# A Mamba group's exponential, logarithm and sum of time steps, each moved one step in a tile pipeline

## The chip, the cores and the metric

One core of one Trainium2 chip runs the whole program. The metric is device time in microseconds. Lower is better.

The core has five engines with queues of their own, each working in order: PE (matrix products, with weight loads "PEld" beside it), DVE (vector operations), ACT (activation functions and copies), POOL (elementwise work and indirect DMAs) and SP (which here only issues DMAs).

## The reference

The program is a decoder of two layers on x of shape 16 x 100 x 256, with a context of 16 x 361 x 192. Layer 0: retention, cross attention, a mixture of 8 experts. Layer 1: Mamba, cross attention, an int8 product. The change lies in the Mamba part:

```
xz = x @ W_in                      # 256 -> z 2048, x 2048, B 64, C 64, dt 32
conv = depthwise causal convolution of width 4 over x, B, C, then silu
dt = softplus(dt_proj + dt_bias)   # per token and head, 32 heads
A = -exp(A_log)
h = exp(A * dt) * h + dt * x_t * B_t        # per head, over 100 tokens
y = C_t . h + D * x_t
y = norm_w * rmsnorm(y * silu(z));  return y @ W_out
```

softplus(v) is computed as max(v, 0) + log(1 + exp(-|v|)). With u = exp(-|v|) and w = 1 + u, the kernel takes log(w) and corrects it by u / (w - 1), with a guard for w = 1.

## The kernel before

**Groups and tiles.** The 16 sequences are 4 groups of 4, so 400 tokens. A group's 2048 inner channels are 16 tiles of 128 channels (2 heads). The loop at L1536 runs over n, from 0 to 72; a tile's group is n // 16, its index i is n % 16. The recurrence is computed as a masked product: per head, a 100 x 100 matrix L of exp of differences of running sums of A * dt, times the products B . C, times dt * x.

**The pipeline.** Within the block that opens at L1514 the order of PE, ACT, DVE, POOL and SP is that of the Python text: what is written first is queued first, on each engine. In step n, in this order: `closing` (end of the group before, i from 5 to 8), `gated` of tile n-4 (POOL, L1387), `rows_of` of tile n+2 (SP reads L's rows, L1316), `exponents` of tile n+1 (POOL, L1324 and L1325), `squares` of tile n-5 (POOL, L1398), `weights` of tile n-2 (DVE, L1332), `project` of tile n (PE L155, ACT L1199, DVE L1204 three times), `silu` of tile n (ACT, L1353 for z, L1354 for x), `exps` of tiles n and n+1 in even steps (ACT, L1328), `square` of tile n-4 (ACT, L1392), `turn` of tile n-2 (PE L1361, DVE `xdt` L1365), `result` of tile n-3 (PE L1379, DVE `y` L1384), `out` of tile n-5 (PE L1407), then `fetch` and `between`. The product `mm` has two PSUM buffers: one for x's half of the projection, one for z's.

**The next group's start.** `between` (L1473) prepares group g+1 in steps of group g, with one PSUM tile `st` for all of it:
- i = 7, 8: `start_x` turns x.
- i = 9: `start_dt` (L1237): PE makes the time steps' projection; DVE adds the bias (`dt_v`, L1248) and takes -|v| (`dt_u`, L1252); ACT takes its exponential (L1253); DVE adds 1 (`dt_w`, L1254); ACT takes the logarithm (`dt_ln`, L1255).
- i = 10: `start_sum` (L1271): eight DVE operations of 100 x 128 (L1274 to L1282), which end in `dt` and `dta` = dt * exp(A_log). Then `start_bc` for B (L1258): a PE product into `st`, an ACT step (L1199 on `bct`) and three DVE operations (L1204 on `bct`) that read `st`.
- i = 11: `start_rows` (L1286): four PE products (L1288) of `dta` with a triangle of ones into `st`, an ACT copy (L1292), a write to DRAM by SP (L1294) that `rows_of` later reads.
- i = 12: `start_cols` (L1296), i = 13: `start_bc` for C, i = 14: silu of B and C.

Group 0 has no group before it: its start runs ahead of the loop (L1515 to L1535).

**Activation tables.** ACT works from a table of functions that a load instruction puts in place; the compiler sets these loads where the function changes. A trace shows them as ACT_TABLE_LOAD under the line of the activation behind them.

Of the kernel before, what the change touches and what calls it, by code (L numbers as in the profile page):

```python
# [33 lines left out]
NG = B // G  # L34
# [48 lines left out]
def bc(ap, axis, n):  # L83

    v = ap.unsqueeze(axis)
    shape = list(v.shape)
    shape[axis] = n
    return v.to_broadcast(shape)


class Net:
# [1116 lines left out]
    def mamba(self, pool, w_out, w_x1):  # L1208
# [10 lines left out]
        one = lambda tag: self.psum.tile([P, 512], F32, tag=tag, name=tag, bufs=1)  # L1219
        xTs, dts, cols, das, gms, ssqs, accs = {}, {}, {}, {}, {}, {}, {}  # L1220
        xcs, szs, xdts, ls, ys, y2s = {}, {}, {}, {}, {}, {}
        st, mid, bct, rows_in, moe, ends = {}, {}, {}, {}, {}, {}
# [3 lines left out]
        def start_x(g, k):  # L1226
            if k == 0:
                st[g] = one("st")
                xTs[g] = pool.tile([P, 2, GT], F32, tag="xT", name="xT")
            for b in range(G):  # L1230
                nc.tensor.transpose(
                    st[g][:, b * T : (b + 1) * T], self.x[g][:, b, k * P : (k + 1) * P],
                    self.ident(T),
                )
            nc.scalar.copy(xTs[g][:, k, :], st[g][:, :GT])

        def start_dt(g):  # L1237

            pd = st[g][:T, :]
            for b in range(G):
                self.mm(
                    pd[:, b * 32 : (b + 1) * 32],
                    [(xTs[g][:, k, b * T : (b + 1) * T], self.w_in[:, k, 4224:4256]) for k in range(2)],
                )
            v, u, w, one, ln = (tile_(f"dt_{n}") for n in ("v", "u", "w", "one", "ln"))
            nc.vector.tensor_tensor(  # L1248
                v, pd[:, : 32 * G].rearrange("t (b h) -> t b h", b=G), bc(self.row("dt_bias"), 1, G),
                ALU.add,  # L1250
            )
            nc.vector.scalar_tensor_tensor(u, v, -1.0, v, ALU.mult, ALU.min)  # L1252
            nc.scalar.activation(u, u, AF.Exp)  # L1253
            nc.vector.tensor_scalar(w, u, 1.0, None, ALU.add)  # L1254
            nc.scalar.activation(ln, w, AF.Ln)  # L1255
            mid[g] = v, u, w, one, ln

        def start_bc(g, j):  # L1258

            lo_w, lo_b = PV["bc_w"][0], PV["bc_b"][0]  # L1260
            pc, at = st[g][:64, :GT], 4096 + 64 * j
            self.mm(pc, [(self.w_in[:, k, at : at + 64], xTs[g][:, k, :]) for k in range(2)])
            acc = pool.tile([64, GT], F32, tag=f"bc{j}", bufs=1, name="bct")
            self.conv(
                acc, pc,
                lambda k: self.pv[:64, lo_w + 4 * j + k : lo_w + 4 * j + k + 1],
                self.pv[:64, lo_b + j : lo_b + j + 1],
            )
            bct[j] = acc

        def start_sum(g):  # L1271

            v, u, w, one, ln = mid.pop(g)
            nc.vector.tensor_scalar(one, w, 1.0, None, ALU.is_equal)  # L1274
            nc.vector.scalar_tensor_tensor(w, w, -1.0, one, ALU.add, ALU.add)
            nc.vector.tensor_tensor(ln, ln, one, ALU.add)
            nc.vector.reciprocal(w, w)
            nc.vector.tensor_tensor(ln, ln, w, ALU.mult)
            nc.vector.tensor_tensor(ln, ln, u, ALU.mult)
            dt, dta = tile_("dt", 2), tile_("dta")  # L1280
            nc.vector.scalar_tensor_tensor(dt, v, 0.0, ln, ALU.max, ALU.add)
            nc.vector.tensor_tensor(dta, dt, bc(self.exp_a, 1, G), ALU.mult)  # L1282
            dts[g] = dt
            return dta

        def start_rows(g, dta):  # L1286
            for b in range(G):
                nc.tensor.matmul(  # L1288
                    st[g][:32, b * T : (b + 1) * T], dta[:, b, :], upper, start=True, stop=True
                )  # L1290
            rows = pool.tile([32, GT], F32, tag="dt_rows", bufs=1, name="dt_rows")
            nc.scalar.copy(rows, st[g][:32, :GT])  # L1292
            das[g] = tc.dram_tile([32, GT], F32, name=f"sums{g}")
            nc.sync.dma_start(das[g], rows)  # L1294

        def start_cols(g, dta):  # L1296
            pc = st[g][:T, : G * 32]
            nc.tensor.matmul(pc, upper, dta.rearrange("t b h -> t (b h)"), start=True, stop=True)
            cols[g] = tile_("cols", 2)
            nc.scalar.copy(cols[g], pc.rearrange("t (b h) -> t b h", b=G))  # L1300
# [12 lines left out]
        def rows_of(n):  # L1313
            g, i = divmod(n, 16)
            ls[n] = pool.tile([T, 2, G, T], F32, tag="L", bufs=7, name="L")
            nc.sync.dma_start(  # L1316
                ls[n].rearrange("s h b t -> s h (b t)"),
                das[g][2 * i : 2 * i + 2, :].unsqueeze(0).to_broadcast([T, 2, GT]),
            )
# [10 lines left out]
        def weights(n):  # L1330
            g = n // 16
            nc.vector.tensor_tensor(ls[n], ls[n], bc(gms[g], 1, 2), ALU.mult)  # L1332
# [53 lines left out]
        def gated(n):  # L1386
            nc.gpsimd.tensor_tensor(ys[n], ys[n], szs.pop(n), ALU.mult)  # L1387
# [85 lines left out]
        def between(n):  # L1473

            g, i = divmod(n, 16)
            if g + 1 >= NG:
                return
            if i == 5:
                moe[1] = self.moments(moe[0])
            if i == 6:  # L1480
                self.normalize(moe[0], *moe[1])
                self.x[g + 1] = moe[0]
            if i == 7:
                start_x(g + 1, 0)
            if i == 8:
                start_x(g + 1, 1)
            if i == 9:
                start_dt(g + 1)
            if i == 10:
                moe[2] = start_sum(g + 1)  # L1490
                start_bc(g + 1, 0)
            if i == 11:
                start_rows(g + 1, moe[2])
            if i == 12:
                start_cols(g + 1, moe[2])
            if i == 13:
                start_bc(g + 1, 1)
            if i == 14:
                silu_bc()

        def silu_bc():
            for j in range(2):
                nc.scalar.activation(bct[j], bct[j], AF.Silu)

        def closing(n):
            g, i = divmod(n, 16)
            if 1 <= g <= NG and 5 <= i < 9:
                (end_sums, end_add, end_moments, end_norm)[i - 5](g - 1)
# [5 lines left out]
        with tc.manual_schedule(engines={E.PE, E.Activation, E.DVE, E.Pool, E.SP}):  # L1514
            start_x(0, 0)  # L1515
            start_x(0, 1)
            start_dt(0)
            dta = start_sum(0)
            project(0)
            start_rows(0, dta)  # L1520
            start_cols(0, dta)
            for n in range(3):
                rows_of(n)

            self.load_mamba_out(w_out)
            silu(0)
            for j in range(2):
                start_bc(0, j)
                project(1 + j)
                silu(1 + j)  # L1530
            silu_bc()
            for n in range(2):
                exponents(n)
            for n in range(-4, 0):
                fetch(n)  # L1535
            for n in range(n_tiles + 9):  # L1536
                within = lambda k: 0 <= n - k < n_tiles
                closing(n)
                if n % 16 == 2 and n < n_tiles:
                    start_gm(n // 16)  # L1540
                if within(4):
                    gated(n - 4)
                if n >= 1 and within(-2):
                    rows_of(n + 2)
                if n >= 1 and within(-1):
                    exponents(n + 1)
                if within(5):
                    squares(n - 5)
                if within(2):
                    weights(n - 2)  # L1550
                if n >= ahead and within(0):
                    project(n)
                    silu(n)
                if n % 2 == 0 and within(0):
                    exps(n)
                    exps(n + 1)
                if within(4):
                    square(n - 4)
                if 4 <= n < 20:
                    scale_out(n - 4)  # L1560
                if n == 6:
                    self.load_cross1(w_x1)
                if within(2):
                    turn(n - 2)
                if within(3):
                    result(n - 3)
                if within(5):
                    out(n - 5)
                fetch(n)
                between(n)  # L1570
# [465 lines left out]
```

## Time and profile before

| | us |
|---|---|
| median of 3 runs (lowest, highest) | 2004.35 (2004.33, 2005.26) |
| the profiled execution | 2004.99 |
| its span | 2003.1 |
| Mamba's last output products (L1407) end | 1267.5 |
| PE busy in the span | 1800.7 |
| ACT busy in the span | 976.4 |
| POOL busy in the span | 683.9 |
| ACT_TABLE_LOAD, mean of one | 1.283 |
| ACT_TABLE_LOAD at L1253 and at L1255 | 4 each |
| ACT_TABLE_LOAD at L1353, at L1328 | 35, 31 |

A row of a timeline reads: start (us from the span's start), duration (us), engine, line, operation, out<-in, shapes, number of merged instructions, and in brackets how long the engine stood idle before it and what released it. A row of a table by stage reads: stretch, its length, then for PE, PEld, DVE, ACT and POOL the busy time and the number of instructions, then PE's granted clock as a share of full speed, the DMA engines' busy share and GB/s.

### The profile page before, as it was taken

The page shows a single profiled execution, that of the slowest core. Times are in us where ns is not written, and L with a number is a line of the kernel's source. Part 1 is how long each engine was busy: PE and PEld are TensorE (multiplying, and loading weights), DVE is VectorE, ACT ScalarE, POOL GpSimd, SP SyncE. Part 2 cuts the span into 40 slices and gives each one's busy share as a digit, 9 for nine tenths or more (in the row PEclk, how much of TensorE's full clock was granted, in tenths as well). Part 3 has the DMA queues.
Part 4 walks back from the last instruction along what each step waited for, and adds up shares of the span by engine and source line. Part 5 has one row for each costly group of instructions (what it writes and reads, how often), then busy time and mean ns, then how long its engine had stood idle before and what let it go on. Part 6 is the DMA issues. An engine that isn't in the chain of part 4 may idle for free. (4 is left out here: it accounts for less than half of the span.)

```text
span 2003.1 us, 31924 instructions
## 1 busy us (share of the span) xinstructions
PE 1800.7 (90%) x12268; PEld 1063.4 (53%) x12268; DVE 1124.8 (56%) x2466; ACT 976.4 (49%) x2294; POOL 683.9 (34%) x501
## 2 busy tenths in 40 slices
PE   6998999999949996799898998899999999999985
PEld 3556556555626663455555555445555555555553
DVE  3454577777632222687878867354446535444554
ACT  5732477667612221577667677333343433344343
POOL 2222232434320001558576566222222322322231
PEclk9999999999869998799999999999999999999997
DMA  4700600101023111422111110000000000000000
GB/s 148 311 1 1 230 24 16 31 26 33 16 87 135 45 45 33 121 103 80 41 57 52 47 52 33 21 16 8 9 8 16 17 8 8 9 16 15 1 9 9
DMA packets 46848, 96.98 MB, mean 48 GB/s; under 512 B 5844, under 2 KB 25940, under 8 KB 44266
## 3 DMA queue, kind: packets, MB, share of 16 engines
q1 hardware_dynamic: 41642, 83.75, 12.3%
q0 software_dynamic: 5056, 11.20, 1.8%
q8 instruction: 98, 1.61, 0.3%
q14 instruction: 52, 0.43, 0.1%
HBM read 69.48 MB, written 25.44 MB: 47 GB/s over the span
## 5 line engine op out<-in xcount | busy, mean ns | idle before, releaser
L1686 POOL TENSOR_TENSOR s<-s,den 100x1444 f32<-100x1444 f32 x64 | 165.9, 2593 | 509.5 <-DVE den L1685 467.7
L1677 ACT ACTIVATE s<-sc,top 100x361 f32<-100x361 f32 x256 | 140.3, 561 | 181.4 <-DVE top L1672 173.4
L155 PE MATMUL mm<-xT,w_mamba_in 128*128 128x400 f32 x512 | 203.2, 542 | 23.2 <-ACT sz L1353 18.9
L605 ACT COPY pT<-tr 128x400 f32<-128x400 f32 (+1 forms) x192 | 94.1, 494 | 190.6 <-PE tr L602 190.2
L1204 DVE SCALAR_TENSOR_TENSOR xc<-mm,pv,xc 128x388 f32<-128x388 f32 (+2 forms) x192 | 119.9, 625 | 80.1 <-ACT xc L1199 75.0
L739 POOL TENSOR_SCALAR w_experts<-w_experts 100x1444 f32<-100x1444 f32 x64 | 88.9, 1388 | 213.8 <-DVE w_experts L735 162.4
L1672 DVE TENSOR_REDUCE top<-sc 100x2 f32<-100x722 f32 x128 | 110.2, 902 | 88.5 <-PE sc L1667 88.5
L747 ACT ACTIVATE w_experts<-w_experts,top 100x361 f32<-100x361 f32 x256 | 149.3, 586 | 21.5 <-POOL w_experts L739 21.3
L155 PEld LDWEIGHTS mm<-xT,w_mamba_in 128*128 128x128 f32 x512 | 100.4, 204 | 107.0 <-ACT sz L1353 27.4
L605 DVE COPY pT<-tr 128x400 f32<-128x400 f32 x192 | 105.1, 569 | 56.7 <-PE tr L602 49.2
L735 DVE TENSOR_SCALAR_CACHE_REDUCE w_experts<-sc 100x361 f32<-100x361 f32 x256 | 121.2, 529 | 14.2 <-PE sc L729 13.5
L602 PEld LDWEIGHTS tr<-cn,s 100*128 100x128 f32 (+1 forms) x768 | 76.1, 154 | 88.5 <-issue 64.4
L1648 DVE COPY v<-mm 128x512 f32<-128x512 f32 (+1 forms) x96 | 61.9, 686 | 107.3 <-PE mm L595 107.3
L155 PE MATMUL sc<-w_experts,e_xT 128*128 x256 | 118.1, 605 | 2.2 <-DMA e_x<-rows 2.2
L602 PE MATMUL tr<-cn,s 100*128 100x100 f32 (+1 forms) x768 | 99.2, 266 | 18.5 <-DVE pT L605 18.5
L1387 POOL TENSOR_TENSOR y<-y,sz 128x400 f32<-128x400 f32 x64 | 67.5, 1055 | 134.1 <-DVE y L1384 103.0
L602 PE MATMUL tr<-cn,w_experts 100*128 100x100 f32 (+1 forms) x768 | 97.2, 267 | 13.6 <-ACT w_experts L747 6.1
L1706 PE MATMUL tr<-pT,v 128*64 128x100 f32 (+1 forms) x1536 | 98.2, 267 | 12.0 <-ACT pT L605 7.2
L1324 POOL TENSOR_TENSOR L<-L,cols 100x800 f32<-100x800 f32 x64 | 99.5, 1555 | 23.5 <-ACT sz L1353 23.5
L1407 PE MATMUL acc<-y,w_mamba_out 128*128 128x400 f32 x256 | 102.4, 524 | 1.6 <-ACT w_mamba_out L1414 1.5
L1631 DVE COPY k<-mm 128x361 f32<-128x361 f32 x128 | 62.4, 529 | 69.7 <-PE mm L595 69.7
L1667 PE MATMUL sc<-k,q 64*100 64x361 f32 x512 | 98.7, 505 | 0.2 <-ACT s L1677 0.2
(298 smaller groups left out, 3618.7 us busy)
## 6 DMA issues: line engine op xcount, KB each, us to landing
L<-sums SPq DMA_DIRECT2D x64, 312.5 KB
rows<-nothing SPq DMA_DIRECT2D x15, 1024.0 KB
w_experts<-in_moe_w_dram SPq DMA_DIRECT2D x24, 512.0 KB
ctx<-in_ctxT_dram SPq DMA_DIRECT2D x32, 361.0 KB
e_x<-rows SPq DMA_DIRECT2D x32, 128.0 KB
rows<-e_y SPq DMA_DIRECT2D x32, 128.0 KB
w_mamba_in<-in_m_w_in_dram SPq DMA_DIRECT2D x1, 2048.0 KB
w_mamba_in<-in_m_w_in_dram POOLq DMA_DIRECT2D x1, 2048.0 KB, 13.8
```

Of the source, the lines that this page charges most:

```text
L155: self.nc.tensor.matmul(out, lhsT, rhs, start=i == 0, stop=i == len(pairs) - 1)
L602: self.nc.tensor.transpose(pt[:n, h * T : (h + 1) * T], probs[:, h, k0 : k0 + n], self.ident(T))
L605: evict(pT[:n, k, :], pt[:n, :GT])
L735: nc.vector.tensor_scalar(s[:, h, :], sc[h // 2][:T, h % 2, :CTX], -1e4, 1e4, ALU.max, ALU.min, accum_out=top[:, h : h + 1],)
L747: nc.scalar.activation(s[:, h, :], s[:, h, :], AF.Exp, bias=top[:, h : h + 1], scale=-1.0, accum_out=dens[b][:, hd : hd + 1],)
L1204: nc.vector.scalar_tensor_tensor(a3[:, :, s:], p3[:, :, : T - s], w(k), a3[:, :, s:], ALU.mult, ALU.add)
L1324: nc.gpsimd.tensor_tensor(ls[n], ls[n], bc(c, 3, T), ALU.subtract)
L1407: nc.tensor.matmul(acc[:, c, :GT], self.w_out[:, i, c * P : (c + 1) * P], y, start=i == 0, stop=i == 15)
L1667: nc.tensor.matmul(sc[h // 2][:T, h % 2, :CTX], qTs[g][i][r0 : r0 + 64, at], kTs[b][i][r0 : r0 + 64, :], start=True, stop=True,)
L1672: nc.vector.tensor_reduce(top[:, 2 * p : 2 * p + 2], sc[p][:T, :, :CTX], AX.X, ALU.max, negate=True)
L1677: nc.scalar.activation(s[:, h, :], sc[h // 2][:T, h % 2, :CTX], AF.Exp, bias=top[:, h : h + 1], accum_out=den[:, h : h + 1],)
L1686: nc.gpsimd.tensor_tensor(s, s, bc(den, 2, CTX), ALU.mult)
```

## The change

`start_dt` is cut into three. The part up to `dt_u` stays in step 9. The exponential and `dt_w` become `start_exp`, at the end of step 10, ahead of B's product, in the place where the sum stood. The logarithm becomes `start_ln`, at the front of step 11, right behind `closing`. The sum moves to the end of step 11, directly ahead of the row products. For group 0 the calls stand in the order that they had.

```diff
             nc.vector.scalar_tensor_tensor(u, v, -1.0, v, ALU.mult, ALU.min)
+            mid[g] = v, u, w, one, ln
+
+        def start_exp(g):
+            v, u, w, one, ln = mid[g]
             nc.scalar.activation(u, u, AF.Exp)
             nc.vector.tensor_scalar(w, u, 1.0, None, ALU.add)
+
+        def start_ln(g):
+            v, u, w, one, ln = mid[g]
             nc.scalar.activation(ln, w, AF.Ln)
-            mid[g] = v, u, w, one, ln
...
             if i == 9:
                 start_dt(g + 1)
             if i == 10:
-                moe[2] = start_sum(g + 1)
+                start_exp(g + 1)
                 start_bc(g + 1, 0)
             if i == 11:
+                moe[2] = start_sum(g + 1)
                 start_rows(g + 1, moe[2])
...
             start_dt(0)
+            start_exp(0)
+            start_ln(0)
             dta = start_sum(0)
...
                 closing(n)
+                if n % 16 == 11 and n // 16 + 1 < NG:
+                    start_ln(n // 16 + 1)
                 if n % 16 == 2 and n < n_tiles:
```

## The prediction, made before the changed kernel was run

> **What bounds the kernel now.** I read the page's first part, then its chain that ended last, and then, because that chain reaches back only to the last stage (its first pieces start near 1270 us), the timelines of each engine around the edited steps of the Mamba stage.
>
> ```profile
> PE 1800.7 (90%) x12268; PEld 1063.4 (53%) x12268; DVE 1124.8 (56%) x2466; ACT 976.4 (49%) x2294; POOL 683.9 (34%) x501
> ```
>
> PE has the program. What the edit is worth must therefore be read as time that PE gains or loses. The edited steps run for group 0 before the pipeline starts (in unchanged order, so nothing changes there) and for groups 1 to 3 inside the tile loop, near 882, 999 and 1115 us. The second is shown; the third repeats its ACT, DVE and POOL rows within 0.1 us, the first has 0.5 us more on ACT per tile. I write tile i for the loop's i = n % 16. First PE: output products of tile 11, the row products of `start_rows`, the projection of tile 12.
>
> ```profile
> 1008.73 1.61 PE L1407 MATMUL acc<-y,w_mamba_out 128*128 128x400 f32 x4
> 1013.24 1.33 PE L1288 MATMUL st<-cn,dta 100*32 100x100 f32 x8 [2.90 <-DVE bct L1204]
> 1014.49 4.11 PE L155 MATMUL mm<-xT,w_mamba_in 128*128 128x400 f32 x8
> ```
>
> PE runs dry at 1010.34 and stands 2.90 us until DVE has finished the B convolution (`bct`). The view of waits for 996 to 1019 us has only this wait and one of 0.6 us before 997.39 on PE. So ACT keeps PE waiting nowhere between 997.39 and 1010.34. Now DVE, from the end of tile 10:
>
> ```profile
> 1004.93 0.62 DVE L1384 SCALAR_TENSOR_TENSOR y<-xc,pv,tr 128x400 f32<-128x400 f32 x1
> 1005.47 0.22 DVE L1274 TENSOR_SCALAR dt_one<-dt_w 100x128 f32<-100x128 f32 x1
> ...
> 1006.73 1.62 DVE L1276 TENSOR_TENSOR dt_ln<-dt_ln,dt_one 100x128 f32<-100x128 f32 x1
> ...
> 1011.18 1.91 DVE L1204 SCALAR_TENSOR_TENSOR bct<-st,pv,bct 64x388 f32<-64x388 f32 x3
> 1013.02 0.97 DVE L1332 TENSOR_TENSOR L<-L,gm 100x800 f32<-100x800 f32 x1
> 1013.91 1.93 DVE L1204 SCALAR_TENSOR_TENSOR xc<-mm,pv,xc 128x388 f32<-128x388 f32 x3
> ```
>
> The sum, eight small operations, takes 1011.18 - 1005.47 = 5.71 us. In group 0, where POOL is quiet, the same eight take 0.23 + 2.58 = 2.8 us (806.40 to 808.98, and the first before it). POOL explains the stretch: its 4.5 us of work per tile start when `y` is done.
>
> ```profile
> 1005.63 1.03 POOL L1387 TENSOR_TENSOR y<-y,sz 128x400 f32<-128x400 f32 x1 [2.40 <-DVE y L1384]
> 1006.62 1.59 POOL L1324 TENSOR_TENSOR L<-L,cols 100x800 f32<-100x800 f32 x1
> 1008.29 0.85 POOL L1325 TENSOR_SCALAR L<-L 100x800 f32<-100x800 f32 x1
> 1009.11 1.03 POOL L1398 TENSOR_TENSOR ssq<-ssq,y 128x400 f32<-128x400 f32 x1
> ```
>
> Each slow DVE operation ends within 0.15 us behind the end of a POOL operation; the last three, after 1010.14, cost 0.29 us.
>
> **What it removes.** ACT now loads four tables around tile 9's end:
>
> ```profile
> 998.57 1.28 ACT L1253 ACT_TABLE_LOAD   x1
> ...
> 1000.25 1.28 ACT L1255 ACT_TABLE_LOAD   x1
> ...
> 1002.45 1.28 ACT L1353 ACT_TABLE_LOAD   x1
> ...
> 1005.05 1.28 ACT L1328 ACT_TABLE_LOAD   x1
> ```
>
> After the edit the exponential stands behind tile 10's own `exps`, whose table is in: the load of L1253 goes. Tile 10's silu follows tile 9's silu: the load of L1353 goes. The logarithm's load moves to the front of tile 11, where the silu load behind it was due anyway. That is 2 x 1.28 = 2.57 us of ACT per group, 6 loads and 7.7 us in all. I credit **nothing** for it, since PE waits for ACT nowhere in that stretch.
>
> The loads stand back to back with their neighbours (one activation ends at 998.55, the load starts at 998.57, its activation at 999.92). The Trainium skill, "ScalarE: Activation LUTs", section "What ACT_TABLE_LOAD costs", puts 1380 ns of drain beside each load, 2.66 us a switch; six would be an estimated 16 us, twice what these rows show. Its rule to batch activations by table set speaks for this change. Either figure is ACT time, and the row decides.
>
> **What it moves.** I follow one group, from ACT free at 998.55.
>
> 1. Tile 10 starts earlier. Its projection is on PE at 997.39 in both cases; the first half is out by 998.9, ACT's convolution step (0.68) by 999.6. DVE has finished `dt_u` at 999.89, does the weights (0.97) and starts the convolution at 1000.85 instead of 1002.47, 1.6 us earlier; `y` is done at 1003.9 instead of 1005.5.
> 2. DVE now does not go on to the sum but to `dt_w`, which waits for the exponential. In the old run ACT needed 1008.31 - 1004.51 = 3.80 us from the second silu to the B step (load, two `exps`, square); 1.6 us earlier, and with 0.33 for the exponential, the B step starts at 1007.0 and ends at 1007.7. DVE stands idle about 3 us, time that the sum filled before. Behind the waiting `dt_w` stands only the B convolution, which needs that later ACT step anyway.
> 3. `dt_w` 0.23 to 1.1 us (its rows with POOL quiet and busy), then the B convolution, 1.84: DVE is through at 1009.5 to 1010.0.
> 4. ACT: logarithm load from 1007.7, logarithm until 1009.3, tile 11's convolution step until 1009.9, in time for DVE. The logarithm's new wait for `dt_w` is covered by its own load; uncovered it would hold ACT's tile 11 by up to 0.5 us.
> 5. Tile 11 on DVE: weights, convolution, `xdt`, `y` took 1016.90 - 1013.02 = 3.88 us. So `y` is done at 1013.4 to 1013.9.
> 6. Then the sum. `y` again releases POOL's 4.5 us, so I take 5.7 us, the row with POOL on, not 2.8. It ends at 1019.1 to 1019.6; PE's row products, which took 0.22 us to follow DVE, start at about 1019.4 instead of 1013.24: **+6.1 us**. PE stops at 1010.34 as before, so its gap grows from 2.9 to 9.0 us.
>
> The sum has thus been taken from a place where DVE would have waited for ACT and put where PE waits for DVE, behind 3.88 us of tile 11.
>
> 7. The clock. After the gap:
>
> ```profile
> 1014.50:1016.00 1.50, 1.50 (x4) 0.84 (x4) 1.43 (x4) 0.06 (x1) 0.00 (x0) 0.50 0.00 0
> ```
>
> The column before the last two is PE's granted clock: half, after a gap of 2.9 us. Rows and projection take 1018.60 - 1013.24 = 5.36 us; undisturbed they are 0.85 + 2.95 less 0.08 overlap = 3.72. So 1.64 are lost today. After the gap of 4.55 us before 981.50 the projection alone took 5.24, a loss of 2.3; after 6.28 us before 837.10, 1.60 and 5.67 for 0.91 and 2.95, a loss of 3.4. I take 2.3, the projection's own row: **+0.65 us** (0 to 1.8).
>
> The Trainium skill, "TensorE: Matmul & The Clock Gate", section "What's actually happening", says that an idle window of about 3.4 us halves the clock, that a busy one restores it, and that the windows run freely. It speaks against the change: a 9 us gap always holds such a window, so an estimated 3.4 to 6.8 us run at half speed, 1.7 to 3.4 lost where 1.64 are now. The trace agrees with the length (half speed from 979.3 to 986.1, 6.8 us).
>
> 8. Not on the path: `start_rows`' write to DRAM and the SP reads queued behind it come later by as much as PE and everything after them, so their lead is kept. No instruction and no DMA is added. Nothing gives the time back: from 1013.24 on PE runs without a wait until 1039.8, where 1.5 us go on ACT's silu of B and C, which itself follows PE.
>
> **Sum.** Per group 6.1 + 0.65 = 6.75, three groups +20 us. On the profiled execution (2004.99 us, of which 2003.1 are span) that gives 2025.2; the median of the runs shown is 2004.35, so I say 2024.5. Bounds: sum in 2.8 us and the clock loss as today, 3.2 x 3 = 10, hence 2014; a loss of 3.4 on the clock, 7.9 x 3 = 24, and 2 for item 3's spread and phases, hence 2030.
>
> **The rivals.**
> - POOL doesn't stretch the sum, since it has run off: 3.2 to 4 per group, 2014 to 2017. For it: group 0. Against: `y` releases POOL at the same point. 14%.
> - Worse: the late rows shift the clock's windows so that further tiles run at half speed, or DVE's tile 12 adds a wait: over 8.5 per group, 2030 to 2038. For it: 6.8 us at half clock near 980. 9%.
> - Not slower: the table loads are what holds the rows. ACT's switches around tile 9 delay the B step, thus the B convolution, thus PE; without them the rows come up to 2.57 us a group earlier, 2004.35 - 7.7 = 1996.7. It decides if the sum is done by 1013.24, that is if `y` of tile 11 is done by 1007.5. Against: that `y` follows a B convolution that can't start before ACT's step ends at 1007.7. 5%. Between, the two cancel within 4 us: 3%.
> - The change doesn't do what it says: a load is placed otherwise, say one before the moved exponential. That costs ACT 1.28 us a group; through items 2 to 6 the rows come 1.3 later, 2028, inside the range.
>
> My forecast has 69%. 0.2%, 4 us, is about what a measurement of this kernel can tell from no change: faster 0.05, same 0.03, slower 0.92. The range 2013 to 2031 leaves out the not slower cases and the worse one.
>
> **What would show it.** Table loads: 6 fewer, none at the exponential in groups 1 to 3. DVE idle 3 us ahead of `dt_w`, released by ACT. The sum still about 5.7 us. PE's wait at the row products about 9 us, released by DVE's `dta` instead of `bct`, and half clock behind it. Wrong: a wait there under 5 us, or a mamba stage that ends earlier though the wait has grown.

## The result, and the profile after

| | before | after |
|---|---|---|
| median, us (lowest, highest) | 2004.34 (2002.94, 2005.26) | 2028.07 (2027.02, 2030.37) |
| ratio, 95% interval | | 1.0113 (1.0101 to 1.0126) |
| the profiled execution, its span | 2004.99, 2003.1 | 2027.02, 2025.1 |
| ACT_TABLE_LOAD at the exponential / at `silu` of z | 4 / 35 | 1 / 32 |
| PE's gap at the row products, groups 1, 2, 3 | 2.73, 2.90, 2.91 | 9.60, 9.68, 9.65 |

The kernel became slower by 1.13%, 23.7 us, at the place and by the mechanism that were forecast. New lines in the file shift the names: the exponential is now L1257, `dt_w` L1258, the logarithm L1262, the sum L1280 to L1288, `y` L1390, the row products L1294.

PE's timeline of the second group in the kernel after; it ends the output products at 1018.44 and waits for `dta`, no longer for `bct`:

```profile
1016.83 1.61 PE L1413 MATMUL acc<-y,w_mamba_out 128*128 128x400 f32 x4
1028.12 1.51 PE L1294 MATMUL st<-cn,dta 100*32 100x100 f32 x8 [9.68 <-DVE dta L1288]
1029.56 3.94 PE L155 MATMUL mm<-xT,w_mamba_in 128*128 128x400 f32 x8
1033.34 0.60 PE L1367 MATMUL tr<-cn,xc 128*100 128x128 f32 x4
```

DVE's timeline in the same stretch:

```profile
1011.25 0.62 DVE L1390 SCALAR_TENSOR_TENSOR y<-xc,pv,tr 128x400 f32<-128x400 f32 x1
1014.96 1.55 DVE L1258 TENSOR_SCALAR dt_w<-dt_u 100x128 f32<-100x128 f32 x1 [3.08 <-ACT dt_u L1257]
1016.43 1.92 DVE L1204 SCALAR_TENSOR_TENSOR bct<-st,pv,bct 64x388 f32<-64x388 f32 x3
...
1022.15 0.22 DVE L1280 TENSOR_SCALAR dt_one<-dt_w 100x128 f32<-100x128 f32 x1
...
1023.41 1.62 DVE L1282 TENSOR_TENSOR dt_ln<-dt_ln,dt_one 100x128 f32<-100x128 f32 x1
...
1027.68 0.29 DVE L1288 TENSOR_TENSOR dta<-dt,exp_a 100x128 f32<-100x128 f32 x1
```

DVE stands 3.08 us between `y` of tile 10 and `dt_w`, does B's convolution and tile 11, and only then, at 1022.15, the sum; with POOL's work beside it again, 5.74 us. POOL in that stretch:

```profile
1022.32 1.03 POOL L1393 TENSOR_TENSOR y<-y,sz 128x400 f32<-128x400 f32 x1 [5.89 <-DVE y L1390]
1023.30 1.59 POOL L1330 TENSOR_TENSOR L<-L,cols 100x800 f32<-100x800 f32 x1
```

L1282 on DVE ends at 1025.03, 0.14 us behind the end of POOL's L1330. And ACT's loads: nothing ahead of the exponential, one ahead of the logarithm, one ahead of tile 11's silu.

```profile
1014.63 0.29 ACT L1257 ACTIVATE dt_u<-dt_u 100x128 f32<-100x128 f32 x1
1014.83 0.67 ACT L1199 ACTIVATE bct<-st,pv 64x400 f32<-64x400 f32 x1
1015.51 1.28 ACT L1262 ACT_TABLE_LOAD   x1
1016.81 0.31 ACT L1262 ACTIVATE dt_ln<-dt_w 100x128 f32<-100x128 f32 x1
...
1017.71 1.28 ACT L1359 ACT_TABLE_LOAD   x1
```

**Where the 22.0 us of span come from.** The gaps grew by 6.87, 6.78 and 6.74, together 20.4 us. From the start of the row products to tile 12's next PE step (`turn`) it took 5.26, 5.20 and 5.21 us before and 6.07, 5.22 and 5.40 after: 1.0 us more, the clock. 0.9 us are there already ahead of the loop's changed steps (one PE line stands at 837.10 before and at 837.99 after) and belong to no step of the change; -0.3 is left.

### The profile page after: what moved, and what is told of

Its sections match the earlier page's. It is cut to its first block, busy times and chain, and to the rows that moved or that the text cites. A ratio compares the mean times of both kernels' runs of the same rounds, so it can differ in the third digit from the quotient of the medians.

```text
span 2025.1 us, 31918 instructions
## 1 busy us (share of the span) xinstructions
PE 1806.8 (89%) x12268; PEld 1067.9 (53%) x12268; DVE 1126.0 (56%) x2466; ACT 969.6 (48%) x2288; POOL 684.6 (34%) x501
## 5 line engine op out<-in xcount | busy, mean ns | idle before, releaser
L1330 POOL TENSOR_TENSOR L<-L,cols 100x800 f32<-100x800 f32 x64 | 99.6, 1556 | 23.4 <-DMA L<-sums 23.3
```

## The experiments

Main theory: PE waits for a sum that DVE reaches too late, behind tile 11, and that POOL stretches. Rivals: DVE's new wait for the exponential; the clock behind the longer gap; the table loads.

| run | median, us | ratio to before on the same chip, 95% interval |
|---|---|---|
| sum alone moved | 2029.49 | 1.0128 (1.0113 to 1.0144) |
| sum at the front of step 11 | 2004.96 | 1.0006 (0.9996 to 1.0015) |
| before, rows one step later | 2001.24 | 0.9984 (0.9975 to 0.9993) |
| 22 products in the gap | 2036.72 | 1.0167 (1.0151 to 1.0183) |
| 11 products in the gap | 2020.86 | 1.0075 (1.0060 to 1.0091) |
| 13 products in the gap | 2020.15 | 1.0069 (1.0056 to 1.0083) |
| the changed kernel again | 2028.03 | 1.0112 (1.0097 to 1.0128) |
| sum ahead of y | 2016.71 | 1.0059 (1.0044 to 1.0075) |
| after, rows one step later | 2008.11 | 1.0012 (0.9998 to 1.0025) |
| exponential ahead of exps | 2000.38 | 0.9982 (0.9973 to 0.9991) |
| the same, rows one step later | 1994.28 | 0.9945 (0.9931 to 0.9958) |

**The sum alone moved.** Exponential and logarithm stay where they were.

```diff
             if i == 10:
-                moe[2] = start_sum(g + 1)
                 start_bc(g + 1, 0)
             if i == 11:
+                moe[2] = start_sum(g + 1)
                 start_rows(g + 1, moe[2])
```

> The kernel before, with one edit: the sum goes from step 10 to step 11, ahead of the row products; exponential and logarithm stay in step 9 with all their table loads. If the sum's place costs the time (main theory): B's convolution on DVE then waits only for ACT's B step, 1008.97 in the kernel before, and ends at 1010.85; tile 11 takes 3.88 us, the stretched sum 5.7, so the row products start at about 1020.6 instead of 1013.24. PE's gap is about 10.3 us, 7.3 more a group, and the time about 2004 + 3 x 7.3 = 2026, or up to 2029 with the clock behind the gap. If DVE's new wait for the exponential in step 10 costs the time (rival): there is none here, so about 2004. If the six table loads are worth anything at all: more than 2028 by up to 7.7.

2029.49 us. The sum's place gives the whole loss without any new wait for the exponential, so that rival falls. DVE stands idle at the same point all the same, for ACT's B step:

```profile
1012.46 0.62 DVE L1384 SCALAR_TENSOR_TENSOR y<-xc,pv,tr 128x400 f32<-128x400 f32 x1
1016.54 1.92 DVE L1204 SCALAR_TENSOR_TENSOR bct<-st,pv,bct 64x388 f32<-64x388 f32 x3 [3.46 <-ACT bct L1199]
```

That is the time that the sum filled in the kernel before. The gaps are 10.57, 10.36 and 10.33 us, 2.3 us more in all than in the changed kernel. That is what moving the exponential and the logarithm brings on balance: without their loads ACT's B step comes 1.6 us a group earlier, and `dt_w`, which then stands ahead of B's convolution, takes about half of that back. The medians are too near each other to tell it (the intervals overlap).

**The sum at the front of step 11.** The changed kernel, with the sum right behind the logarithm.

```diff
                 if n % 16 == 11 and n // 16 + 1 < NG:
                     start_ln(n // 16 + 1)
+                    moe[2] = start_sum(n // 16 + 1)
...
             if i == 11:
-                moe[2] = start_sum(g + 1)
                 start_rows(g + 1, moe[2])
```

> The changed kernel, with one edit: the sum stands at the front of step 11, right behind the logarithm, ahead of tile 11's work on DVE. Main theory: B's convolution ends at the same place as in the changed kernel (10.2 us behind the point that was 1000 in the kernel before), POOL is quiet by then, so the sum takes 2.8 us and not 5.7; the row products start at about 1013.3 in the clock of the kernel before, PE's gap is about 3 us, and the time is 2003 to 2006. Rival (the wait for the exponential is to blame): that wait of 3.1 us per group stays, so the time stays above 2018. Rival (nothing but the sum's length matters, wherever it stands): 2028 - 3 x 2.9 = 2019.

2004.96 us, as the main theory said: everything else of the change is kept, and the loss is gone. Its DVE:

```profile
1008.02 1.53 DVE L1258 TENSOR_SCALAR dt_w<-dt_u 100x128 f32<-100x128 f32 x1 [3.08 <-ACT dt_u L1257]
1009.48 1.92 DVE L1204 SCALAR_TENSOR_TENSOR bct<-st,pv,bct 64x388 f32<-64x388 f32 x3
1011.32 0.21 DVE L1280 TENSOR_SCALAR dt_one<-dt_w 100x128 f32<-100x128 f32 x1
...
1011.85 0.28 DVE L1282 TENSOR_TENSOR dt_ln<-dt_ln,dt_one 100x128 f32<-100x128 f32 x1
...
1014.22 0.98 DVE L1338 TENSOR_TENSOR L<-L,gm 100x800 f32<-100x800 f32 x1
```

The wait for the exponential is still 3.08 us; the sum takes 2.90 (1011.32 to 1014.22), since POOL's tile ended at 1009.48. PE's gaps are 2.89, 2.95 and 1.53. The third is short because PE came late and not because the sum came early: tile 10's projection took 4.65 us there instead of 2.95, at half clock.

**The sum ahead of y.** The changed kernel, with the sum in step 11 between tile 11's convolution and `turn`.

```diff
+                if n % 16 == 11 and n // 16 + 1 < NG:
+                    moe[2] = start_sum(n // 16 + 1)
                 if within(2):
                     turn(n - 2)
...
             if i == 11:
-                moe[2] = start_sum(g + 1)
                 start_rows(g + 1, moe[2])
```

> The changed kernel, with one edit: in step 11 the sum stands on DVE behind tile 11's convolution and ahead of xdt and y, so that y, which releases POOL's next tile, comes behind it. If POOL's work beside the sum stretches it from 2.8 to 5.7 us (main theory): the sum takes 2.8 to 2.9 us and starts 1.1 us earlier, PE's gap shrinks from 9.65 to about 5.6 us, and the time is 2028 - 3 x 4 = 2016. If the sum is slow in the loop for another reason (rival): 5.7 us again, gap 8.5, 2024 to 2025.

2016.71 us. Only `xdt`, `y` and with `y` POOL's release went behind the sum. DVE and then POOL:

```profile
1016.90 0.22 DVE L1280 TENSOR_SCALAR dt_one<-dt_w 100x128 f32<-100x128 f32 x1
...
1017.36 0.28 DVE L1282 TENSOR_TENSOR dt_ln<-dt_ln,dt_one 100x128 f32<-100x128 f32 x1
...
1019.73 0.68 DVE L1371 TENSOR_TENSOR xdt<-tr,dt 100x512 f32<-100x512 f32 x1
```

```profile
1021.03 1.03 POOL L1393 TENSOR_TENSOR y<-y,sz 128x400 f32<-128x400 f32 x1 [8.72 <-DVE y L1390]
```

The sum takes 2.83 us, and L1282 falls from 1.62 to 0.28. PE's gaps are 5.56, 5.62 and 5.61, 4.0 less a group. Of these, 2.9 are the stretch and 1.1 the two DVE operations; so some 8.7 us of the change's cost come from POOL beside the sum.

**The rows one step later**, in the kernel before and in the kernel after, so that PE has tile 12 ahead of them. The edit is shown for the kernel before; in the kernel after the sum stays in step 11.

```diff
-            if i == 11:
+            if i == 12:
                 start_rows(g + 1, moe[2])
-            if i == 12:
+            if i == 13:
                 start_cols(g + 1, moe[2])
-            if i == 13:
+            if i == 14:
                 start_bc(g + 1, 1)
-            if i == 14:
+            if i == 15:
                 silu_bc()
```

> The kernel before, with the row products one step later (12), column products in 13, C's product in 14, its silu in 15. If PE's gap of 2.9 us and the half clock behind it are a loss of their own, that can be had by giving PE other work: 4.5 us less a group, 1991. If DVE is what holds this stretch (it works without a break from 1002.5 to 1022 there), PE meets the same delay at the projection of tile 12, whose second half needs the buffer that tile 11's convolution reads until 1015.84: 2000 to 2004.

> The changed kernel, with row products one step later (12), column products in 13, C's product in 14, its silu in 15; the sum stays at the end of step 11 with POOL's work beside it. If the loss is PE standing behind a sum that has just begun (main theory): PE does the projection, turn, result and output of tile 12 meanwhile, about 7.2 us of the 9.65, and waits 1 to 3.5 us in pieces; DVE, which takes tile 12's convolution behind the stretched sum, holds it by 1 to 2 us a group against the kernel before: 2007 to 2012. If the sum's lateness can't be hidden, since DVE's chain runs through it: above 2020.

Before with this edit: 2001.24. The gap doesn't vanish; it goes to the second half of tile 12's projection, whose buffer DVE's convolution of tile 11 still reads:

```profile
1012.96 1.61 PE L155 MATMUL mm<-xT,w_mamba_in 128*128 128x400 f32 x4 [1.07 <-ACT sz L1353]
1017.44 2.16 PE L155 MATMUL mm<-xT,w_mamba_in 128*128 128x400 f32 x4 [2.88 <-DVE xc L1204]
```

So in the kernel before it is mainly DVE, with the sum of 5.7 us in its queue, that holds this stretch, and the wait at the rows is only where it shows. After with this edit: 2008.11, as expected; 20 of 24 us come back by letting PE go on during the sum. The rest can't be told from zero against the kernel before. Against the kernel before with the same edit, 2001.24, the move still costs 5 to 6 us by the ratios: the two intervals don't overlap, and PE still waits 2.30, 2.45 and 2.42 us for `dta`.

**Products in the gap.** The changed kernel, with matrix products into `st` ahead of the rows, overwritten by them, so that PE's clock stays up.

```diff
         def start_rows(g, dta):
+            if g:
+                self.mm(st[g][:, :GT], [(self.w_in[:, 0, :P], xTs[g][:, 0, :])] * 13)
```

> The changed kernel, with 22 matmuls of 128x400 ahead of the row products in groups 1 to 3, whose result is overwritten: 8.1 us of PE work that fit into the gap of 9.65 us. If the gap itself is the loss and the clock only a small part: the rows start where they did, but at full clock; rows and projection take 3.7 us instead of 5.2 to 6.1, so 1.5 to 2.4 less a group, 2021 to 2024. If the slower clock behind the longer gap makes most of the difference between the two kernels (rival): about 2008. If neither: 2028.

> The run with matmuls in the gap again, with half as many: a 128x400 product in 32-bit floats is two matmuls of 0.34 us, so that 22 products took 15 us and not 8. 11 products are 7.5 us, from the end of the output products to 2 us ahead of dta. If the gap is the loss and the clock a part of 1.5 to 2.3 us a group: rows at the same place, rows and projection in 3.7 us instead of 5.2 to 6.1, about 2022. If the clock makes most of the difference between the two kernels: about 2008. If the clock makes none: 2028.

> As the run with 11 products in the gap, with 13: 26 matmuls of 0.34 us are 8.8 us, so that PE stands only about 0.6 us ahead of the row products, in place of 1.9, after which the clock fell to half all the same in the profiled execution. If the clock behind the gap costs what its rows show: rows and projection in 3.7 us instead of 5.2 to 6.1 in each group, 5 to 6 us less than the changed kernel. If it costs nothing in the end (PE waits for others by then): the same as the changed kernel.

> The changed kernel itself, on the same chip as the run with 13 products, for a fair comparison with it and a second look at its gaps: 2024 to 2031.

22 products were a miss: they are 44 matmul records of 15.0 us, so the rows came 5.3 us later than `dta` allowed, and 2036.72 says nothing of the clock. 11 products gave 2020.86, but the profiled execution shows half clock behind the remaining 1.9 us in all three groups (rows to `turn` in 5.29, 5.25 and 5.29 us), so that it doesn't say where the gain came from. 13 products settle it:

```profile
901.84 0.87 PE L1296 MATMUL st<-cn,dta 100*32 100x100 f32 x8 [0.57 <-DVE dta L1288]
902.64 2.95 PE L155 MATMUL mm<-xT,w_mamba_in 128*128 128x400 f32 x8
905.43 0.60 PE L1369 MATMUL tr<-cn,xc 128*100 128x128 f32 x4
```

Rows to `turn` in 3.59 us, in the other two groups 3.59 and 3.60: 5.9 us less than in the changed kernel's profile. 2020.15 against 2028.03 on the same chip is 7.9 less; the 2 us between lie within the intervals. So half clock costs the changed kernel about 6 us; but by the same rows it costs the kernel before 5.26 + 5.20 + 5.21 - 3 x 3.59 = 4.9, and explains 1 us of the difference. That rival falls too.

**A better order.** The run with the sum at the front, with the exponential ahead of step 10's two `exps` (the table load that stood ahead of them then stands ahead of it), and the weights of step 11 moved into DVE's idle time in step 10; then the same with the rows one step later.

`start_exp` then holds the activation alone, and `end_exp` is `dt_w`.

```diff
             if i == 10:
-                start_exp(g + 1)
+                weights(n - 1)
+                end_exp(g + 1)
                 start_bc(g + 1, 0)
...
-                if within(2):
+                if within(2) and not (n % 16 == 11 and n // 16 + 1 < NG):
                     weights(n - 2)
...
+                if n % 16 == 10 and n // 16 + 1 < NG:
+                    start_exp(n // 16 + 1)
                 if n % 2 == 0 and within(0):
                     exps(n)
```

> The run with the sum at the front of step 11, with the exponential ahead of step 10's two exps on ACT instead of behind the square, and tile 9's weights on DVE at the end of step 10, ahead of dt_w. DVE's wait for the exponential was 3.1 us there; it shrinks to about 1, filled by the weights. If DVE's chain up to dta sets the row products: dta 1.2 to 2 us earlier a group and tile 11's convolution 2 us earlier, so the gap of 2.9 us falls to 1 to 1.7, 1996 to 2001. If something else holds PE there: 2004 to 2005.

> The kernel of the run before this one, with row products one step later (12), column products in 13, C's product in 14, its silu in 15. If PE's remaining wait is only for dta: it vanishes behind the projection of tile 12, 1 to 3 us a group less, 1993 to 1998. If DVE's work in the stretch is the bound: no different from the run before, within 3 us.

2000.38 and 1994.28 us. The first lies in its range, but its gaps don't: they are 2.41, 2.07 and 0.38 us, where 1 to 1.7 was expected, and the third is again short because tile 10's projection ran at half clock (4.65 us). The second beats the kernel before by 0.55%. In it DVE waits 0.24 us for the exponential and 0.96 for the B step where it waited 3.08, and the sum runs in 2.90:

```profile
1002.80 0.98 DVE L1341 TENSOR_TENSOR L<-L,gm 100x800 f32<-100x800 f32 x1
1004.01 1.56 DVE L1261 TENSOR_SCALAR dt_w<-dt_u 100x128 f32<-100x128 f32 x1 [0.24 <-ACT dt_u L1257]
1006.53 1.92 DVE L1204 SCALAR_TENSOR_TENSOR bct<-st,pv,bct 64x388 f32<-64x388 f32 x3 [0.96 <-ACT bct L1199]
1008.38 0.21 DVE L1283 TENSOR_SCALAR dt_one<-dt_w 100x128 f32<-100x128 f32 x1
...
1011.28 1.94 DVE L1204 SCALAR_TENSOR_TENSOR xc<-mm,pv,xc 128x388 f32<-128x388 f32 x3
```

What is left on PE are two waits of 1.1 us at tile 12's projection, and the rows start at 1017.63 without any.

## Why the prediction was right, step by step

The forecast was 2024.5 in 2013 to 2031; measured 2028.07. Times of the second group, the profile after set back by 8.09 us (tile 9's convolution starts at 1003.64 instead of 995.55):

| item | forecast | measured |
|---|---|---|
| 1. `y` of tile 10 done | 1003.9 | 1003.8 |
| 2. ACT's B step starts; DVE idle | 1007.0; 3 | 1006.7; 3.08 |
| 3. `dt_w`; B's convolution done | 0.23 to 1.1; 1009.5 to 1010.0 | 1.55; 1010.2 |
| 5. `y` of tile 11 done | 1013.4 to 1013.9 | 1014.1 |
| 6. the sum; rows start; gap | 5.7; 1019.4; 9.0 | 5.74; 1020.0; 9.68 |
| 7. clock, per group | +0.65 | +0.81, +0.02, +0.19 |
| per group; three groups | 6.75; 20 | 7.1 on average; 21.4 |

- **The loads.** Six fewer, three at the exponential and three at silu, as forecast. The prediction credited nothing for them, but its items 1 and 2 carry the B step that comes earlier without them; the run with the sum alone moved puts the worth of this at 2.3 us in its gaps, net of `dt_w`'s new place. ACT's busy time fell by 6.8 us (976.4 to 969.6) while the kernel grew by 23.7.
- **The move.** Right in each link. The mis-sized term is `dt_w`: it was bounded by its rows in the kernel before, at most 1.1 us, but lay across two POOL operations here and took 1.55. That is most of the 0.7 us by which the gap was underrated; the rest is in item 6 itself, where a sum that ends at 1019.1 to 1019.6, with 0.22 behind it, gives 1019.3 to 1019.8 and not 1019.4.
- **The stretch of the sum.** I took 5.7 and not 2.8 because `y` would release POOL at the same moment; the run with the sum ahead of `y` (2.83 us) shows that to be the cause.
- **The clock.** Overrated: +0.65 a group was taken, 0.34 on average came. The stretch at half clock did grow, from 3.4 us a group to 10.2 (in the second group from 1013.4 to 1016.9 before, from 1021.4 to 1031.6 after), but most of it fell into the gap, where PE had nothing to do. Behind the gap's end PE worked at half clock for 3.4 us before and for 5.2, 3.5 and 3.8 us after, within the 3.4 to 6.8 us that item 7 gives as the other estimate.
- **What bounds it.** One sentence of the prediction was too narrow: PE "has the program". In this stretch of the kernel before, DVE holds PE: through `bct` at the rows, and with the rows one step later through tile 11's convolution, 2.88 us ahead of the second half of tile 12's projection. Item 6 is right because the sum sits in DVE's queue ahead of whatever PE waits for.
- **The size.** 21.4 us are accounted for in the profile, 23.7 lie between the medians; the ratio's interval, 1.0101 to 1.0126, is 20 to 25 us. Part of the nearness is luck: the gap was taken 0.7 us a group too small in its growth, the clock 0.3 too large, and the two errors partly cancel.

## What to carry to other kernels

Count a moved step at its new place by what stands ahead of it in its engine's queue and by who waits behind it: here 6.8 us of ACT were saved and 23.7 us lost, because eight small DVE operations left a place where their engine would have waited anyway and came to stand right ahead of a PE wait. Ask also what runs beside the new place: put just behind the operation that releases POOL, the sum took 5.7 us, and just ahead of it 2.8. When a gap appears on the busy engine, first give that engine the next piece of independent work (20 of the 24 us came back), then look for where the wait has gone.

## What the runs showed of the hardware that was not expected

The clock's drop doesn't follow from the length of the gap alone, and it came behind gaps shorter than the 3.4 us of idle time that item 7 of the prediction reckons with: behind 2.9 us in the kernel before and 1.9 in the run with 11 products. Behind a gap of 1.53 us (third group of the run with the sum at the front, row products at 1131.96) the clock stayed full; behind one of 0.81 us it fell. That is the run with 13 products, second group, ahead of tile 10; the column before the last two is the clock:

```profile
1000.00:1001.30 1.30, 0.51 (x6) 0.40 (x5) 1.23 (x3) 1.25 (x2) 0.19 (x1) 1.00 0.00 0
1001.30:1003.00 1.70, 1.68 (x4) 0.96 (x5) 1.67 (x5) 0.96 (x2) 0.35 (x1) 0.70 0.00 0
1003.00:1005.00 2.00, 2.00 (x5) 1.01 (x4) 2.00 (x3) 0.68 (x1) 2.00 (x2) 0.50 0.00 0
```

The projection there took 4.65 us instead of 2.95, for 0.81 us of waiting. In the second group of the run with the sum at the front, an equal wait of 0.81 us at the same place left the clock full, and the projection took 2.95. What decides between such cases was not tried and stays open.
